# Layer 0's transposed features made in the last step of the first pipeline stage, in two buffers, instead of in the first step of the second stage

## The chip, the cores and the metric

The kernel runs on one core of a Trainium2 chip. The metric is the device time in microseconds (us), the median of several executions. The core has a matrix engine (PE), a vector engine (DVE), a scalar engine that evaluates functions from tables (ACT), GpSimd (POOL, used here only at the start), and queues that issue DMA transfers (SP's queue, in this kernel). Each engine works through its own list of instructions in the order in which the built program has them, and waits on semaphores where it needs another engine's result.

## The reference

Sixty-four graphs of 256 nodes with 128 features (`x`: 64 x 256 x 128) and dense 0/1 adjacency matrices (`adj`: 64 x 256 x 256) go through four message-passing layers, each followed by a residual and a layer norm:

```python
x = _layernorm(x + _L0_gnn_ref(x, adj, W, b))
x = _layernorm(x + _L1_gnn_ref(x, adj, ...))
x = _layernorm(x + _L2_gnn_ref(x, adj, ...))
x = _layernorm(x + _L3_gnn_ref(x, adj, ...))
```

Layer 0, the one the change is in, computes for each node the maximum over its neighbours of a pair term, with the weight matrix cut in two halves of 128 rows:

```python
W1, W2 = (W[:d], W[d:])
p = jnp.einsum('bnd,do->bno', x, W1 - W2)
q = jnp.einsum('bnd,do->bno', x, W2)
pre = p[:, :, None, :] + q[:, None, :, :] + b
h = jax.nn.relu(pre) * adj[..., None]
return jnp.max(h, axis=2)
```

Layer 1 has three projections with ELU (which needs Exp), two aggregations over the adjacency matrix and a Tanh. Layer 2 is a two-step graph convolution with ELU. Layer 3 forms a message for each pair of neighbours, with a layer norm (a square root) and a Gelu, and sums them. So four functions that ACT takes from tables occur: Exp, Tanh, Sqrt and Gelu.

## The kernel before, in words

The kernel does not visit all 256 x 256 pairs. It sorts each graph's neighbour lists into 40 "slots" of falling width, 4800 columns in all (`WIDTH`), and gathers a neighbour's vector by a matmul with a one-hot matrix `hot` (128 x 4800, for each of the two halves `h` of the nodes). Layer 0 takes the maximum over slots, layer 3 the sum. Because `hot` is a matrix of zeros and ones, the fp32 vectors are cut into three bf16 parts (`split3`, giving `q3` in layer 0 and `c3` in layer 3) that are multiplied one after the other into the same PSUM tile `bigp`. A second, general path stands behind a branch that these inputs do not take.

The work on one graph is cut into four stages, each a Python generator:

- `first`: loads `x0` and the adjacency `an`, sorts, makes `perm`, `permT`, `rank`, `lack` and, last, the one-hot matrix `hot`;
- `second`: layer 0 (`layer_0`), then layer 1 (`Shared.layer_1`);
- `third`: layer 2, then the first part of layer 3 (`c3`, `dT`, and the first four pieces by `sums_of`);
- `last`: the rest of layer 3 by pieces of 1024 columns (the fifth piece of each half has 704), the Gelu, the sums over slots, the final update and the store.

Four graphs are in flight at a time: while graph u is in `last`, u+1 is in `third`, u+2 in `second` and u+3 in `first`. The helper `together` interleaves the steps of the four generators (a step ends at each `yield`) in proportion to the numbers in `STAGES`. The Tile framework then schedules the recorded instructions onto the engines: it decides the order of each engine's list itself, within the data dependencies and the buffers that are free, so a moved step can shift every engine's order. All 64 graphs are unrolled; the order repeats from graph to graph in one "round" per graph. Function tables of ACT are loaded (`ACT_TABLE_LOAD`) wherever two functions of different tables follow each other in ACT's final order; the profile puts each load on the line of the function that needs it.

Names and lines that matter (numbers of the profile):

- `to_features` (L205, L207): two transposes on PE into a PSUM tile, then a copy by ACT into a tile in SBUF. It makes `xT_0`, `xT_1`, `xT_2` (layers 0, 1, 2; the profile shows all three as `xT`) and `x3T`.
- `layer_0`: L650 multiplies the features by `w0qp` (both weight halves); L497 to L500 cut q in three; L668 and L684 gather into `bigp`; L686 and L492 take the maximum into `lanes`; L691 ends a half (`total_m`), L694 and L695 transpose it (`mk`, twice a graph); L702 to L712 finish the layer.
- `layer_1`: feature copy, L221 and L228 the projections, L192 the Exp of `io` (two projections) and of `nd` (the third), L236 and L238 the aggregations, L241 their copy `ag`, L247 the update, L252 the Tanh.
- Layer 3: L731 gathers into `bigp`, L735 adds `dT` and gives `pre`, L739 squares, L746 sums the squares on PE, L748 copies `row`; two pieces of `row` go to DRAM and back as `vr` (L753, L765), L72 and L73 take the inverse root, L774 and L835 spread it as `rs_s`. In `last`, L846 multiplies `pre` by `rs_s`, L848 applies the Gelu, L492 and L488 fold the slots into `sums`, L867 to L869 multiply by the update weights, L872 copies the result (`ak`, once for each half), L877 brings it back to node order.
- Layer norms: L169 to L178 on DVE with the Sqrt of `rs` at L72 on ACT.
- Prologue: weights are loaded by `load` (L77) and in `prep` (L126 to L152); `sparse` counts slots with chains of small DVE instructions (L414 to L424), in scratch memory that is given back before the graphs' buffers are set up there.

## Time and profile before

| | |
|---|---|
| median of 3 runs | 5589.18 us (5588.3 to 5589.55) |
| the profiled execution | 5585.87 us, of which the trace spans 5583.8 |
| TensorE clock granted, mean | 0.876 |
| rounds | L798, once a graph, from 44.0 to 5423.0 us |
| one round by its stations (start, us) | `mk` 2604.88; layer 1's feature copy 2621.17; Exp of `io` 2626.39; second `ak` 2629.35; Tanh 2638.18; layer 0's feature copy 2640.81; `q` 2645.70; `lanes` 2649.08; next `mk` 2686.68 |

The round in the table and the one before it, by window (us busy; the windows run from the second `mk` of a graph to the first `lanes` of the next, and from there to the next second `mk`):

| window | length | PE | DVE | ACT | granted clock |
|---|---|---|---|---|---|
| 2519.04 to 2566.44 | 47.40 | 38.56 | 38.82 | 38.95 | 0.83 |
| 2566.44 to 2604.88 | 38.44 | 31.43 | 35.81 | 26.93 | 0.94 |
| 2604.88 to 2649.08 | 44.20 | 35.42 | 38.54 | 38.86 | 0.94 |
| 2649.08 to 2686.68 | 37.60 | 30.59 | 35.80 | 26.91 | 0.94 |

In the profile's lines, a group gives the line, the engine, the operation, the tile written and the tiles read with their shapes, the count, then the busy time in us, the mean of one in ns, and the idle time of the engine just before. A wait is given as the waiting engine, tile and line, then what it waited for, then the total in us, the count and the longest. A timeline row gives the start in us, the duration, the engine and line, and in brackets the idle time before it with what ended it. PEld is the load of a weight matrix into PE, which overlaps the matmuls. DVE is 92 to 95% busy between `lanes` and the next `mk`, and 82 to 87% busy between `mk` and `lanes`.

### The profile page before, as it was taken

The page shows a single profiled execution, that of the slowest core. Times are in us where ns is not written, and L with a number is a line of the kernel's source. Part 1 is how long each engine was busy: PE and PEld are TensorE (multiplying, and loading weights), DVE is VectorE, ACT ScalarE, POOL GpSimd, SP SyncE. Part 2 cuts the span into 40 slices and gives each one's busy share as a digit, 9 for nine tenths or more (in the row PEclk, how much of TensorE's full clock was granted, in tenths as well). Part 3 has the DMA queues.
Part 4 walks back from the last instruction along what each step waited for, and adds up shares of the span by engine and source line. Part 5 has one row for each costly group of instructions (what it writes and reads, how often), then busy time and mean ns, then how long its engine had stood idle before and what let it go on. Part 6 is the DMA issues. An engine that isn't in the chain of part 4 may idle for free.

```text
span 5583.8 us, 83622 instructions
## 1 busy us (share of the span) xinstructions
PE 4511.0 (81%) x27408; PEld 2487.9 (45%) x27408; DVE 4805.5 (86%) x14654; ACT 4218.5 (76%) x6465; POOL 2.0 (0%) x10
## 2 busy tenths in 40 slices
PE   5888888888788888887887888888888878888884
PEld 3444444444444444444444444444444444444442
DVE  7788888898888888888988888889888888888886
ACT  2777777777777777777777777777777777777776
POOL 0000000000000000000000000000000000000000
PEclk8888888888888888888888888888888888888886
DMA  0212222222222122222222222221222222212212
GB/s 24 65 59 72 67 63 66 72 65 66 66 65 70 60 72 67 63 66 74 63 66 67 70 66 61 69 67 63 71 70 63 66 67 70 66 59 71 64 59 76
DMA packets 292814, 365.17 MB, mean 65 GB/s; under 512 B 151952, under 2 KB 210448, under 8 KB 292368
## 3 DMA queue, kind: packets, MB, share of 16 engines
q1 hardware_dynamic: 292368, 359.73, 20.8%
q8 instruction: 218, 3.57, 0.3%
q14 instruction: 228, 1.87, 0.1%
HBM read 345.07 MB, written 14.53 MB: 64 GB/s over the span
## 4 chain that ended last, share of the span: by engine, by line
PE 42%; DVE 34%; ACT 17%; issue 5%; DMA 3%; SPq 0%; DVEq 0%; POOL 0%; ACTq 0%; POOLq 0%
PE bigp L731 8%; PE bigp L668 8%; DVE lanes L492 8%; DVE pre L735 6%; ACT L72 6%; DVE hot L628 5%; DVE sums L492 5%; PE mm L867 4%; DVE pre L846 3%; PE mm L746 3%; PE mm L877 2%; PE mm L817 2%; PE mm L294 2%; DMA rs_s<-scale_line 2%; ACT sums L848 2%
## 5 line engine op out<-in xcount | busy, mean ns | idle before, releaser
L668 PE MATMUL bigp<-hot,q 128*128 128x512 fp8e4 (+1 forms) x3840 | 1117.5, 391 | 206.2 <-DVE lanes L492 179.7
L731 PE MATMUL bigp<-hot,c 128*128 128x512 fp8e4 (+1 forms) x3840 | 1010.6, 395 | 136.0 <-DVE pre L735 77.1
L735 DVE TENSOR_TENSOR pre<-bigp,dT 128x512 f32<-128x512 f32 (+6 forms) x1664 | 841.4, 534 | 252.2 <-PE bigp L731 245.9
L739 ACT ACTIVATE sq<-pre 128x1024 f32<-128x1024 f32 (+1 forms) x640 | 636.6, 995 | 273.2 <-DVE rs L73 196.9
L492 DVE TENSOR_TENSOR lanes<-bigp,lanes 128x512 f32<-128x512 f32 (+6 forms) x1536 | 769.3, 501 | 12.2 <-ACT vr L72 2.9
L846 DVE TENSOR_TENSOR pre<-pre,rs_s 128x1024 f32<-128x1024 f32 (+1 forms) x640 | 734.4, 1148 | 35.6 <-DMA rs_s<-scale_line 34.5
L492 DVE TENSOR_TENSOR sums<-pre,sums 128x1024 f32<-128x1024 f32 (+6 forms) x1024 | 628.3, 614 | 11.6 <-ACT pre L848 11.2
L848 ACT ACTIVATE pre<-pre,be,g 128x1024 f32<-128x1024 f32 (+1 forms) x512 | 600.0, 1172 | 11.0 <-DVE pre L846 6.9
L731 PEld LDWEIGHTS <-c 128*128 128x128 bf16 x3840 | 346.2, 102 | 544.5 <-issue 268.1
L848 ACT ACT_TABLE_LOAD x447 | 573.5, 1283 | 7.9
L72 ACT ACT_TABLE_LOAD x447 | 573.5, 1283 | 7.9
L748 ACT ACTIVATE row<-mm,eps_t 128x256 f32<-128x256 f32 (+1 forms) x640 | 293.5, 459 | 361.9 <-PE mm L746 351.0
L668 PEld LDWEIGHTS <-q 128*128 128x128 bf16 x3840 | 309.6, 100 | 514.9 <-DVE lanes L492 186.5
L746 PE MATMUL mm<-sq,ones 128*32 128x256 f32 (+1 forms) x5120 | 436.5, 418 | 113.7 <-ACT sq L739 110.7
L628 DVE TENSOR_SCALAR hot<-rank 128x512 fp8e4<-128x512 bf16 (+5 forms) x1536 | 485.4, 345 | 0.0
L684 PEld LDWEIGHTS <-pick 42*128 42x128 bf16 x2944 | 154.5, 95 | 449.6 <-issue 435.2
L650 PE MATMUL mm<-w0qp,xT 128*128 128x256 f32 x256 | 130.0, 662 | 266.3 <-ACT xT L207 266.3
L867 PE MATMUL mm<-w3u,sums 128*128 128x128 f32 x2048 | 293.8, 287 | 44.9 <-DVE sums L492 44.9
L867 PEld LDWEIGHTS mm<-w3u,sums 128*128 128x128 f32 x2048 | 258.7, 195 | 75.9 <-PE bigp L731 39.6
L684 PE MATMUL bigp<-lack,pick 42*128 42x36 bf16 (+16 forms) x2944 | 275.8, 187 | 0.0
L746 PEld LDWEIGHTS mm<-sq,ones 128*32 128x32 f32 x5120 | 107.2, 115 | 352.5 <-ACT sq L739 162.0
L73 DVE RECIPROCAL vr<-vr 128x16 f32<-128x16 f32 (+1 forms) x320 | 79.5, 249 | 161.7 <-ACT vr L72 161.6
(227 smaller groups left out, 7319.0 us busy)
## 6 DMA issues: line engine op xcount, KB each, us to landing
rs_s<-scale_line SPq DMA_DIRECT2D x512, 512.0 KB
rs_s<-scale_line SPq DMA_DIRECT2D x128, 352.0 KB
an<-in_adj SPq DMA_DIRECT2D x64, 256.0 KB
x<-in_x SPq DMA_DIRECT2D x64, 128.0 KB
line<-row SPq DMA_DIRECT2D x512, 4.0 KB
out<-o SPq DMA_DIRECT2D x64, 128.0 KB
fu<-fulls SPq DMA_DIRECT2D x192, 4.0 KB
vr<-line SPq DMA_DIRECT2D x192, 8.0 KB
```

Of the source, the lines that this page charges most:

```text
L72: nc.scalar.activation(t, t, AF.Sqrt)
L492: nc.vector.tensor_tensor(lanes[:, :k, :w], src[:, i:i + k], lanes[:, :k, :w], op)
L628: nc.vector.tensor_scalar(hot[:, :, at:at + w], rank[:, :, :w], s0 + i + 1.0 - FAR, None, ALU.is_equal, saturate=False)
L668: nc.tensor.matmul(pt[:, :tl], q3[:, i, h], hot[:, h, t0:t0 + tl], start=i == 0, stop=False)
L684: nc.tensor.matmul(o_, l_, r_, start=False, stop=i == len(todo) - 1)
L731: nc.tensor.matmul(pt[:, :bl], c3[:, k, h], hot[:, h, t0 + b:t0 + b + bl], start=k == 0, stop=k == 2)
L735: nc.vector.tensor_add(block(pre[:, b:], n, w, at), block(pt, n, w, at), widen(dT[:, h, :w], n))
L739: nc.scalar.activation(sq[:, :tl], pre[:, :tl], AF.Square)
L746: nc.tensor.matmul(pr[q * Q:(q + 1) * Q, :tl // 4], ones[:, :Q], v4[:, :, q], start=True, stop=True)
L846: nc.vector.tensor_mul(pre[:, :tl], pre[:, :tl], rs[:, :tl])
L848: nc.scalar.activation(msg[:, :tl], pre[:, :tl], AF.Gelu, bias=be3, scale=g3)
L867: nc.tensor.matmul(pt[:, cols], lanes[:, k, cols], w3u[:, 1], start=k == 0, stop=False)
```

## The change

The call of `to_features` for layer 0 moves from the first step of `layer_0` to the end of `first`, after the last instructions that make `hot`. The `yield` that followed it goes away, so `second` has one step fewer, while the weights in `STAGES` stay. The tile `xT_0` gets the two buffers of its pool instead of one. To make room for the second buffer, the raw weights `w0` move from the pool of constants into `prep`, which is given back after the prologue; their load and the two DVE instructions that read them move with them, behind the loads and transposes of layer 1's weights.

```diff
-    w0 = load(l0_w.rearrange("(c p) o -> p c o", p=P), [P, 2, P], "w0")
     w0qp = consts.tile([P, 2, P], F32, name="w0qp")
-    nc.vector.tensor_copy(w0qp[:, 0], w0[:, 1])
-    nc.vector.tensor_sub(w0qp[:, 1], w0[:, 0], w0[:, 1])
...
             lambda t: [(w1_updT[:, c], t[:, c]) for c in range(3)],
         )
+        w0 = prep.tile([P, 2, P], F32, name="w0")
+        nc.sync.dma_start(w0, l0_w.rearrange("(c p) o -> p c o", p=P))
+        nc.vector.tensor_copy(w0qp[:, 0], w0[:, 1])
+        nc.vector.tensor_sub(w0qp[:, 1], w0[:, 0], w0[:, 1])
         w3 = prep.tile([P, 2, P], F32, name="w3")
...
             s["hot"] = hot
+            s["xT"] = sh.to_features(xn, "xT_0")
 
         def layer_0(s):
 
-            xn, hot, lack, lack_t, permT = (s[n] for n in ("xn", "hot", "lack", "lack_t", "permT"))
-            xT = sh.to_features(xn, "xT_0", 1)
-            yield
+            xn, xT, hot, lack, lack_t, permT = (s[n] for n in ("xn", "xT", "hot", "lack", "lack_t", "permT"))
             pq = psum()
```

## The prediction

> **What bounds the kernel now.** I read the page's parts on busy time, then the table-load groups of ACT (the groups by form: busy us, mean ns, idle before), then the waits, then a timeline of ACT at the place the change touches.

> ```profile
> PE 4511.0 (81%) x27408; PEld 2487.9 (45%) x27408; DVE 4805.5 (86%) x14654; ACT 4218.5 (76%) x6465; POOL 2.0 (0%) x10
> ...
> PE 42%; DVE 34%; ACT 17%; issue 5%; DMA 3%; SPq 0%; DVEq 0%; POOL 0%; ACTq 0%; POOLq 0%
> ```

> No engine is full; the chain that ended last hops between PE, DVE and ACT. So the time is set by waits between in-order queues, and an order of instructions matters as much as their number.

> ```profile
> L72 ACT ACT_TABLE_LOAD x447 | 573.5, 1283 | 7.9
> L848 ACT ACT_TABLE_LOAD x447 | 573.5, 1283 | 7.9
> ...
> L192 ACT ACT_TABLE_LOAD x133 | 170.6, 1283 | 2.4
> ...
> L252 ACT ACT_TABLE_LOAD x63 | 80.8, 1283 | 1.1
> L196 ACT ACT_TABLE_LOAD x61 | 78.3, 1283 | 1.1
> ```

> ACT changes its function table 1152 times (these five and one at L426), 1478 us in all, a third of its busy time: Sqrt (L72), Gelu (L848), Exp (L192, L196) and Tanh (L252) alternate.

> ```profile
> PEld mm L650 <- ACT xT L207: 277.5, 64, 4.8
> PE mm L650 <- ACT xT L207: 266.3, 64, 4.5
> DVE pre L735 <- PE bigp L731: 245.9, 308, 2.4
> ACT sq L739 <- DVE rs L73: 196.9, 62, 3.5
> ```

> The second line is what the change aims at: once for each of 64 graphs, layer 0's first matmul (L650) waits 266.3 / 64 = 4.2 us for the copy of its transposed features. The timeline shows why:

> ```profile
> 2636.39 0.47 ACT L748 ACTIVATE row<-mm,eps_t 128x256 f32<-128x256 f32 x1 [0.77 <-PE mm L746]
> 2636.88 1.28 ACT L252 ACT_TABLE_LOAD   x1
> 2638.18 0.42 ACT L252 ACTIVATE y<-y 128x256 f32<-128x256 f32 x1
> 2638.61 1.28 ACT L72 ACT_TABLE_LOAD   x1
> 2639.90 0.33 ACT L72 ACTIVATE rs<-rs 128x2 f32<-128x2 f32 x2
> 2640.14 0.77 ACT L739 ACTIVATE sq<-pre 128x704 f32<-128x704 f32 x1
> 2640.81 0.35 ACT L207 COPY xT<-mm 128x256 f32<-128x256 f32 x1
> ```

> PE finished the transposes at 2636.69 (timeline of PE), but the copy stands behind a Tanh, two table loads, two Sqrts and a Square.

> [...] L748 ends at 2636.86, the load starts at 2636.88, ends at 2638.16, and the Tanh starts at 2638.18. I go by the trace: 1.32 us a switch, plus about 0.1 us because neighbours without a load overlap by that much (the copy at 2640.81 starts 0.10 before the Square ends). [...]

> **The change, part by part.** No arithmetic is added: the built programs have the same number of PE, DVE, POOL and SP instructions. What changes is the order, since layer 0 has one step fewer and the first stage a longer last one, and the scheduler lays all engines out anew. (Line numbers here are those of before.) From the third or fourth graph on, both built orders repeat exactly. A round has 18 table loads before and 22 after; in the branch that runs, 1152 loads become 1383 (the other 134 belong to the branch not taken). 231 x 1.28 = 296 us of ACT work, about 330 with gaps. The rest of ACT's work is unchanged.

> *The aimed-at wait.* In the new order the transposes still stand directly ahead of L650 on PE, after all of the previous round, so they are not made early. On ACT their copy comes straight after the Tanh, ahead of the Sqrt load, the two Sqrts and the Square: 2640.81 would become about 2638.5, 2.3 of the 4.2 us. Also the first cut of q (L497) now stands ahead of the next Gelu. That is the gain, if everything before it came at its old time: 63 x 2.3 = 145 us.

> *Where the four loads lie.* Two lie in layer 2's end (Gelu of the 704 piece between the Sqrt of `vr` and that of `rs`). There ACT idles now (1.72 and 3.20 us around 2597 to 2601, in the timeline), and DVE takes up `rs` only after a dozen other instructions: I cost them at nothing; if that cover is gone, 2 x 1.4 = 2.8 us a round. The other two lie in layer 1. Before: Gelu load, Gelu 1024, feature copy, Gelu 704, then Exp load, Exp of `io`, Exp of `nd`. After: feature copy, Square, `ak`, Gelu load, Gelu 1024, Exp load, Exp `io`, Gelu load, Gelu 704, Square, Exp load, Exp `nd`. Queued behind are the second `ak` copy (L872), `ag` (L241), Tanh, and then the copy of the features itself.

> *The round laid out by hand*, with the durations of the round that begins with the second `mk` copy (L695, 2604.88, called 0). Each instruction of the new order starts when its queue and its inputs allow. Stations, us, before (trace) and after (worked out): layer 1's feature copy 16.3, 15.3; Exp of `io` 21.5, 21.7; end of the Gelu of the 704 piece 17.5, 25.0 (it waits for Exp of `io`, then a load of 1.28 and 0.97 of its own). Its sums on DVE need 3.0 more, with the `pre` additions that stand between (28.0); the sixteen passes of L867 on PE 2.3 (30.3); so the second `ak` is at 30.4 instead of 24.5. PE now does L236 and L238 first (2.3), then L323 and L877 (2.9, to 35.5); L746 0.6, ACT's `row` and Square, L247, L746, `row` (38.8), Tanh load: Tanh 40.1 instead of 33.3. Feature copy 40.5 instead of 35.9: later, although it has less ahead of it. L650 takes 2.1; q 43.0 instead of 40.8. Then come Sqrt load, `rs`, `aT`, `row`, Gelu load, Gelu, Sqrt load, `vr`, and only then `lanes`: 50.0 instead of 44.2. The first fold of `lanes` on DVE is at 51.3 instead of 45.2. DVE has by then done one L846 more (1.2) and `vr` (0.2), so 4.7 us of the 6.1 remain for the round.

> From `lanes` to the next `mk` the old round takes 37.6 us, DVE busy 35.8 of them (busy time by window). The new order leaves DVE 1.4 less there and ACT about 33 instead of 26.9: DVE still limits, so nothing is won back or lost.

> *From one round to all.* That round is a quick one (81.8). The copies L798 run from 44.0 to 5423.0 us, 63 intervals of 85.4; usual rounds lose most of the rest between `mk` and `lanes`, where the granted clock is 0.83 instead of 0.94 and PE is busy 38.6 instead of 35.4 us (windows of the round before). If ACT's longer queue hides all of that, the new round is 81.8 + 4.7 = 86.5, or 1.1 more; if none, 4.7 more. I take 3.0 as the middle: 63 x 3.0 = 189 us.

> *The prologue.* `w0` is now loaded 22 issues later on the SP queue (0.45 us each), after layer 1's weights, and its two DVE instructions (0.5 us) stand behind layer 1's transposed copies. Before, DVE filled the wait for these weights with the first chain of slot counts (L417: 0.31 + 1.07 + 5.73 + 3.28 = 10.4 us, from 1.5 to 12.3, while the first weights came at 15.0). In the new order that chain stands after the copies, ahead of the first graph's loads, which wait for this scratch memory to be freed (the issue at 31.95 waits for DVE, L440): 10.4 us once, nothing covers it. The later `w0` costs nothing by itself, as L650 needs it at 47.8.

> *Other edits.* Two buffers instead of one for the features, and the scratch place of `w0`, run no instruction: nothing.

> Sum: the profiled execution took 5585.9 us (span 5583.8 and 2.1 around it). 5585.9 + 189 + 10 = 5785; the median of the three runs is 3.3 higher, so 5788, which I round to 5790. Ends: 63 x 1.1 + 10 = 79, or 5668; 63 x 4.7 + 10 = 306, or 5895.

> **Rivals.** *Faster.* The wait goes and the loads hide: ACT idles 85.4 - 64.3 = 21 us a round (64.3 is its mean busy time over three rounds, by window), and a wait that ends last is shortened by 2.3; the chain passes at `q` L497 into L668. 5589 - 145 + 10 = 5454. Against: the two loads in layer 1 stand ahead of the very copy that should come sooner. 11 in 100.
> *A wash.* My reading of layer 1 is too strict, and what q gains is given back on DVE, where its second and third cuts now stand behind L846, which waits for the fetched scales: 5589 + 10 = 5599, give or take 40. 11 in 100.
> *All on the path.* ACT ends last everywhere: 4 x 1.4 = 5.6 us a round, 353 + 10: 5952. For: 33 busy us of 37.6 after `lanes` leave little slack. Against: the slack seen in layer 2. 10 in 100.
> *That the change doesn't do what it says* is in the forecast: the transposes still come last before L650.

> **Numbers.** Forecast 68 in 100 at 5790, by itself 5668 to 5895. The range reaches down over most of the wash and up into the last rival: 5590 to 5930; below lie 11 + 4, above 5. A measurement of this kernel can tell about 0.2% (11 us). Faster by more: 11 + 2 = 0.13; within: 0.05, from the wash; slower: 0.82.

> **What would show it.** About 1383 table loads in ACT, still of 1283 ns; the wait of L650 for the features cut to half or less; L798 at 87 to 90 us intervals; the second `ak` later against `mk` by some 6 us; the first `an` load some 10 us later. It is wrong if rounds are 85 or shorter though the loads are there: then the loads lay in slack.

## The result, and the profile after

The changed kernel takes 5624.19 us (median of 6 runs, 5616.19 to 5658.51); the kernel before, on the same chip, 5589.29. The ratio is 1.0072, 95% interval [1.0059, 1.0085]: slower by 0.7%, or 35 us, where 5790 was forecast. The profiled execution is the longest of the six (5658.51 us, span 5656.6), 72.6 us above the profiled one before. The ratios here and below use the runs within 1.5% of the fastest run of the same kernel; this leaves out only ten of the twenty runs of warm_after12.

Up to L640 the lines of the changed kernel are one higher than before (the feature copy L207 is L208, the Exp L192 is L193); from layer 0's first matmul on (L650) they are the same. From the page, busy time of each engine and the chain of work that ended last, by engine:

```profile
PE 4529.3 (80%) x27408; PEld 2565.6 (45%) x27408; DVE 4833.6 (85%) x14654; ACT 4536.5 (80%) x6696; POOL 1.8 (0%) x10
...
PE 43%; DVE 31%; ACT 18%; issue 6%; DMA 2%; SPq 0%; DVEq 0%; ACTq 0%
```

ACT is busy for 318 us more, the other two for 18 and 28. Where ACT's time went, from the groups by line (busy us, mean ns, idle before):

```profile
L848 ACT ACT_TABLE_LOAD x563 | 722.3, 1283 | 10.1
L72 ACT ACT_TABLE_LOAD x502 | 644.1, 1283 | 9.9 <-DMA vr<-line 0.9
L193 ACT ACT_TABLE_LOAD x253 | 324.6, 1283 | 4.6
L253 ACT ACT_TABLE_LOAD x62 | 79.5, 1283 | 1.1
```

With L197 (2) and L427 (1) these are the 1383 loads that the prediction counted. The waits (us in total, times, longest):

```profile
PE mm L694 <- DVE total_m L691: 353.4, 64, 5.6
DVE aT L276 <- PE mm L237: 219.9, 111, 4.5
...
PE mm L746 <- ACT sq L739: 186.8, 69, 6.7
...
PE mm L650 <- ACT xT L208: 139.3, 64, 3.0
...
DVE pre L735 <- PE bigp L731: 66.7, 134, 1.9
```

The wait that the change aims at fell from 4.2 to 2.2 us a round, and DVE's wait for L731 from 245.9 to 66.7 us. In their place L694 stands for 5.5 us a round (before: 1.7), L746 for 2.9 (1.7), and DVE has a new wait at L276.

The 72.6 us divide so. The copy L798 of the first graph starts at 54.86 us instead of 43.95: 10.9 us in the prologue. The 63 intervals of L798 average 86.32 us instead of 85.38: 63 x 0.98 = 62. The median run has 35 - 11 = 24 us for the rounds, 0.4 us each.

**What the average hides.** Before, nearly every round is 85.1 to 85.6 us long. After, rounds of 86.9 and 87.2 alternate (L798 intervals), with rounds of 81.8 and 84.7 between. Most are close to multiples of one time: 85.3 / 25 = 3.41; 81.8 / 24 = 3.41; (86.9 + 87.2) / 51 = 3.41. It is the step of TensorE's clock, as the traces show below. Here is a usual round of before and a round of after, each cut in four from the second `mk` copy (0 to 13 us, 13 to 36, 36 to 52, rest). Columns: window, its length, busy time of PE, weight load, DVE, ACT and POOL, then PEclk, the clock granted to PE, as a share of full speed.

```profile
2348.40:2361.40 13.00, 11.96 (x67) 8.97 (x66) 12.24 (x36) 12.70 (x18) 0.00 (x0) 0.90 0.29 80
2361.40:2384.40 23.00, 18.20 (x121) 11.56 (x119) 19.63 (x69) 16.40 (x24) 0.00 (x0) 0.93 0.14 34
2384.40:2400.40 16.00, 13.74 (x66) 5.69 (x67) 10.76 (x30) 13.60 (x26) 0.00 (x0) 0.68 0.37 113
2400.40:2433.70 33.30, 26.29 (x180) 12.44 (x179) 31.88 (x96) 23.19 (x36) 0.00 (x0) 0.94 0.22 62
```

```profile
2802.20:2815.20 13.00, 9.99 (x52) 6.65 (x50) 13.00 (x40) 12.07 (x17) 0.00 (x0) 0.88 0.13 32
2815.20:2838.20 23.00, 20.18 (x112) 14.31 (x111) 15.37 (x42) 15.90 (x21) 0.00 (x0) 0.78 0.13 39
2838.20:2854.20 16.00, 12.99 (x96) 6.55 (x95) 13.92 (x51) 14.09 (x25) 0.00 (x0) 1.00 0.28 79
2854.20:2888.20 34.00, 26.64 (x183) 12.19 (x175) 32.38 (x97) 29.21 (x44) 0.00 (x0) 0.94 0.31 91
```

Before, the clock is low in the third piece (0.68), right behind the wait of L650. After, that piece has the full clock, and the second has 0.78. In windows of 1 us the clock is 1.00 or 0.50 with at most one mixed window between, so 0.68 of 16 us means 10.2 us at half clock. Over 57 rounds of each profiled run (the sixth to the last but one), us at half clock in a round, by piece:

| kernel | mean round | 0 to 13 | 13 to 36 | 36 to 52 | after 52 |
|---|---|---|---|---|---|
| before | 85.3 | 2.6 | 3.4 | 10.1 | 4.2 |
| after, all | 86.6 | 5.6 | 7.5 | 2.0 | 4.1 |
| after, rounds of 86 (26) | 86 | 3.2 | 9.8 | 0.1 | 4.6 |
| after, rounds of 88 (23) | 88 | 9.1 | 6.4 | 3.9 | 3.7 |
| after, rounds of 82 (2) | 82 | 2.4 | 0 | 0 | 4.3 |
| before, round of 82 (1) | 82 | 2.1 | 0 | 3.4 | 4.6 |

(These rounds run from `mk` to `mk`; one of 86 and one of 88 make two L798 intervals of 87. Six more rounds of after are of 85 or 87.) In the middle pieces the stretches of a single round come as 0, 3.4, 6.8 or 10.2. Before, the usual round has 10.1 us more of them than the quick one and is 3.5 us longer (85.3 against 81.8). The change removed 8.1 us of half clock behind L650 and brought 4.1 behind another gap and 3.0 at the start of the round, where PE comes out of its wait at L694. The total fell, from 20.3 to 19.2 us, and yet the round grew by 1.3: what counts is how far each order is from its own quick round. Before is 10.2 us of half clock and 3.5 us of time above it, after 12.5 and 4.8, so a microsecond at half clock goes with 0.34 and 0.39 us of the round. With the half clock at its least, both orders take 81.8.

The other gap, with its cause, in the timelines of ACT and of PE for the same round (start, duration, engine, line, instruction; in brackets the idle time before and who ended it):

```profile
2818.28 1.28 ACT L848 ACT_TABLE_LOAD   x1
2819.58 1.24 ACT L848 ACTIVATE pre<-pre,be,g 128x1024 f32<-128x1024 f32 x1
2820.84 1.28 ACT L193 ACT_TABLE_LOAD   x1
2822.14 0.63 ACT L193 ACTIVATE elu_e<-io 128x512 f32<-128x512 f32 x1
2822.67 0.46 ACT L748 ACTIVATE row<-mm,eps_t 128x256 f32<-128x256 f32 x1
2823.15 1.28 ACT L848 ACT_TABLE_LOAD   x1
2824.44 0.98 ACT L848 ACTIVATE pre<-pre,be,g 128x704 f32<-128x704 f32 x1
2825.32 1.04 ACT L739 ACTIVATE sq<-pre 128x1024 f32<-128x1024 f32 x1
```

```profile
2826.42 1.08 PE L746 MATMUL mm<-sq,ones 128*32 128x256 f32 x8 [2.82 <-ACT sq L739]
...
2912.55 0.64 PE L746 MATMUL mm<-sq,ones 128*32 128x256 f32 x8 [2.82 <-ACT sq L739]
```

Two of the new loads are among the three that stand ahead of the Square, and PE waits 2.82 us for it. The second PE line is the same place one round on, a round of 81.8 us: the wait is the same 2.82, but the matmuls behind it take 0.64 us and not 1.08. With the same wait that round is no longer than before's quick one; what differs is whether the half clock follows.

**Which gaps slow the clock.** In the traces of before and after the granted clock changes only on a grid with a step of 3.41 us: of the 392 and 362 stretches of one clock, all but the last of each are a whole number of steps long. (The expectations call a step a window.) These are the two PE gaps of 2.82 us cut on that grid, in the columns of above: the one that ends at 2826.42, then the one that ends at 2912.55.

```profile
2822.42:2825.84 3.42, 1.18 (x8) 0.48 (x6) 3.35 (x9) 3.39 (x5) 0.00 (x0) 1.00 0.00 1
2825.84:2829.25 3.41, 2.83 (x16) 1.98 (x16) 3.39 (x16) 3.38 (x5) 0.00 (x0) 0.50 0.00 0
2829.25:2832.66 3.41, 3.41 (x15) 2.53 (x14) 0.34 (x2) 0.61 (x3) 0.00 (x0) 0.50 0.03 4
```

```profile
2907.76:2911.17 3.41, 1.97 (x11) 0.87 (x9) 3.41 (x8) 3.37 (x5) 0.00 (x0) 1.00 0.00 1
2911.17:2914.58 3.41, 1.98 (x19) 1.27 (x19) 3.34 (x14) 3.38 (x6) 0.00 (x0) 1.00 0.02 5
2914.58:2918.00 3.42, 3.42 (x22) 2.99 (x22) 1.83 (x9) 2.94 (x6) 0.00 (x0) 1.00 0.03 4
```

The first gap leaves PE busy for 1.18 of the 3.42 us of a step, and the next steps have half clock, three in all. The second is split by the grid: PE is busy for 1.97 and 1.98 us of the two steps, over half of each, and the clock stays. Nearly all steps of the 57 rounds at full clock agree. In before, PE is less than half busy in 170 of them, and half clock follows all 170; it follows none of the other 915. In after it follows 154 of 161, and 5 of the other 965. At this wait alone, after has 53 gaps of 2.7 to 2.9 us: 48 leave a step with PE at most 0.39 busy, and half clock follows every one; 5 are split with at least 0.54 in both steps, and it follows none. The gap of 4.3 us at L650 before is longer than a step: in each of the 57 rounds it leaves a step with PE at most 0.23 busy, and half clock follows every one. But a gap need not be as long as a step: 2.82 us was enough in those 48 cases of 53, and 2.2 us, what is left of the wait of L650 in after, in 26 of 56. For how long the clock then stays low (mostly 3.4 to 10.2 us) I have no such rule.

### The profile page after: what moved, and what is told of

Same layout as the page of the kernel before. It is cut to its first block, busy times and chain, and to the rows that moved or that the text cites. A ratio compares the mean times of both kernels' runs of the same rounds, so it can differ in the third digit from the quotient of the medians.

```text
span 5656.6 us, 83740 instructions
## 1 busy us (share of the span) xinstructions
PE 4529.3 (80%) x27408; PEld 2565.6 (45%) x27408; DVE 4833.6 (85%) x14654; ACT 4536.5 (80%) x6696; POOL 1.8 (0%) x10
## 4 chain that ended last, share of the span: by engine, by line
PE 43%; DVE 31%; ACT 18%; issue 6%; DMA 2%; SPq 0%; DVEq 0%; ACTq 0%
PE bigp L668 8%; PE mm L867 6%; DVE lanes L493 5%; PE mm L746 5%; DVE hot L629 5%; DVE pre L735 4%; PE bigp L731 4%; DVE sums L493 4%; ACT L848 3%; DVE pre L846 3%; ACT L193 3%; ACT sq L739 2%; PE mm L237 2%; PE mm L702 2%; PE mm L877 2%
## 5 line engine op out<-in xcount | busy, mean ns | idle before, releaser
L668 PE MATMUL bigp<-hot,q 128*128 128x512 fp8e4 (+1 forms) x3840 | 1084.5, 374 | 137.4 <-DVE lanes L493 80.9
L731 PE MATMUL bigp<-hot,c 128*128 128x512 fp8e4 (+1 forms) x3840 | 917.6, 375 | 13.4 <-DVE pre L735 12.8
L735 DVE TENSOR_TENSOR pre<-bigp,dT 128x512 f32<-128x512 f32 (+6 forms) x1664 | 843.0, 536 | 71.8 <-PE bigp L731 66.7
L739 ACT ACTIVATE sq<-pre 128x1024 f32<-128x1024 f32 (+1 forms) x640 | 640.9, 1001 | 226.3 <-DVE rs L73 137.3
L846 DVE TENSOR_TENSOR pre<-pre,rs_s 128x1024 f32<-128x1024 f32 (+1 forms) x640 | 731.5, 1152 | 24.5 <-DMA rs_s<-scale_line 23.5
L848 ACT ACT_TABLE_LOAD x563 | 722.3, 1283 | 10.1
L72 ACT ACT_TABLE_LOAD x502 | 644.1, 1283 | 9.9 <-DMA vr<-line 0.9
L746 PE MATMUL mm<-sq,ones 128*32 128x256 f32 (+1 forms) x5120 | 475.7, 420 | 187.2 <-ACT sq L739 186.8
L848 ACT ACTIVATE pre<-pre,be,g 128x1024 f32<-128x1024 f32 (+1 forms) x512 | 602.5, 1177 | 15.5 <-DVE pre L846 9.0
L731 PEld LDWEIGHTS <-c 128*128 128x128 bf16 x3840 | 344.0, 100 | 413.3 <-issue 91.0
L668 PEld LDWEIGHTS <-q 128*128 128x128 bf16 x3840 | 297.5, 98 | 475.0 <-issue 164.2
L748 ACT ACTIVATE row<-mm,eps_t 128x256 f32<-128x256 f32 (+1 forms) x640 | 290.8, 454 | 217.0 <-PE mm L746 216.7
L867 PE MATMUL mm<-w3u,sums 128*128 128x128 f32 x2048 | 395.8, 349 | 18.3 <-DVE sums L493 17.9
L867 PEld LDWEIGHTS mm<-w3u,sums 128*128 128x128 f32 x2048 | 342.2, 249 | 83.7 <-DVE sums L493 46.3
L694 PE MATMUL mm<-ident,total_m 128*128 128x128 f32 x256 | 68.4, 360 | 353.4 <-DVE total_m L691 353.4
L193 ACT ACT_TABLE_LOAD x253 | 324.6, 1283 | 4.6
L746 PEld LDWEIGHTS mm<-sq,ones 128*32 128x32 f32 x5120 | 114.8, 114 | 372.1 <-ACT sq L739 219.9
```

The lines of the kernel that those rows point to most:

```text
L72: nc.scalar.activation(t, t, AF.Sqrt)
L193: nc.scalar.activation(e, t, AF.Exp)
L668: nc.tensor.matmul(pt[:, :tl], q3[:, i, h], hot[:, h, t0:t0 + tl], start=i == 0, stop=False)
L731: nc.tensor.matmul(pt[:, :bl], c3[:, k, h], hot[:, h, t0 + b:t0 + b + bl], start=k == 0, stop=k == 2)
L735: nc.vector.tensor_add(block(pre[:, b:], n, w, at), block(pt, n, w, at), widen(dT[:, h, :w], n))
L739: nc.scalar.activation(sq[:, :tl], pre[:, :tl], AF.Square)
```

## The experiments

Theories. *Clock*: the old order loses time to the half clock behind L650; the change takes that away and pays by opening other gaps. *Loads*: the change pays with 231 more table loads on the path. *Prologue*: the place of `w0` carries the cost.

| run | median us | ratio to before, 95% |
|---|---|---|
| w0_late | 5599.87 | 1.0020 [1.0013, 1.0027] |
| move_only | 5610.01 | 1.0045 [1.0028, 1.0062] |
| after_keep_step | 5623.29 | 1.0069 [1.0052, 1.0086] |
| before_one_table | 5363.35 | 0.9599 [0.9583, 0.9615] |
| after_one_table | 5394.34 | 0.9651 [0.9634, 0.9667] |
| warm_before12 | 5527.93 | 0.9897 [0.9880, 0.9913] |
| warm_before20 | 5506.08 | 0.9850 [0.9834, 0.9867] |
| warm_after12 | 5572.39 | 0.9908 [0.9883, 0.9932] |
| after_add_pool | 5683.00 | 1.0172 [1.0155, 1.0189] |
| warm_before20_8 | 5725.33 | 1.0251 [1.0234, 1.0269] |
| warm_after_sums | 5734.82 | 1.0236 [1.0185, 1.0286] |

**The change in two halves.** w0_late is before with only the move of `w0`; its instruction order within the rounds is that of before.

```diff
-    w0 = load(l0_w.rearrange("(c p) o -> p c o", p=P), [P, 2, P], "w0")
...
+        w0 = prep.tile([P, 2, P], F32, name="w0")
+        nc.sync.dma_start(w0, l0_w.rearrange("(c p) o -> p c o", p=P))
```

> The kernel before with one part of the change alone: the load of layer 0's weight and its two conversions stand in the preparation behind layer 1's weights, the features stay where they were. If the shifted instruction order makes the rounds longer and w0's place only delays the first stage (10.9 us in the trace of after), the median is 5589 + 11 = 5600 us and the rounds stay at 85.3 us. If the later w0 costs nothing because later work takes up the slack, 5589.

Measured +12.0 us, rounds 85.4. move_only is the other half: `w0` stays, the features move, with one buffer. Its order within the rounds is that of after.

```diff
             s["hot"] = hot
+            s["xT"] = sh.to_features(xn, "xT_0", 1)
...
-            xT = sh.to_features(xn, "xT_0", 1)
-            yield
```

> The other part alone: the features are made at the end of the first stage and the step is dropped, with one buffer, and w0 stays where it was. Theory that the two costs simply add: the median excess of 34.9 us less the prologue's 10.9, so 5613 us, with single runs anywhere from 5605 to 5650 and rounds of 85.5 to 86.5 us. Rival: the place of w0 carried nearly all of it, and the move itself is neutral: 5589 +- 5. Second rival: one buffer instead of two holds the copy back in the first stage and brings a wait there: above 5630.

Measured +22.2 us. The halves add to 34.2 of 34.9, so the second buffer is worth nothing that these runs can tell (the interval of move_only is 10 us to either side), and the rounds carry about 22 us, 0.35 each.

**Are the loads the price?** after_keep_step is after with the dropped `yield` put back at the head of layer 0.

```diff
             xn, xT, hot, lack, lack_t, permT = (s[n] for n in ("xn", "xT", "hot", "lack", "lack_t", "permT"))
+            yield
             pq = psum()
```

> The change, but with the step (the yield) at the head of layer 0 kept, so that layer 0 advances as it did before while the features are made a stage earlier. This order has 1288 activation-table loads in the program instead of 1517, so the two extra loads in layer 1 and the two in layer 2's end are gone. If the extra loads (4 x 1.28 us a round) are what the change pays with, this is faster than the kernel before: the rounds are 85.3 us or less, 5480 to 5600 us. If the length of a round is set by TensorE's half-clock stretches, the loads matter only where they open a gap on TensorE, and the rounds lie near 81.9 (5385 us) or 85.3 (5600 us), whichever number of 3.41-us windows fits, with little in between.

The trace has 1154 loads (1288 less the 134 of the branch not taken) in place of 1383, yet the time is that of the change. So the extra loads come with the dropped step, but they are no needed part of the cost. This run has a third order, though, with little half clock in the middle (1.0 and 3.8 us) and rounds of 85.6 on average, so it has slower spots of its own. Its rounds are of 84, 85 and 87 us, not of the two lengths that were expected: not every order keeps to whole steps of the clock. The cleaner test keeps each kernel's order: after it is laid out, the four functions are replaced by Identity, so the results are no longer those of the network. The replaced instructions take about as long as before (L848: 1172 ns on average in before, 1176 in before_one_table; ACT's busy time falls by 1496 us, of which the 1151 loads that went make 1477).

```diff
+            if type(i).__name__ == "InstActivation" and i.func in (AF.Gelu, AF.Exp, AF.Tanh, AF.Sqrt):
...
+                todo[k] = mybir.InstActivation(func=AF.Identity, **kw)
```

> The kernel before in its own instruction order, with Gelu, Exp, Tanh and Sqrt computed as Identity (this changes the values of the whole network, nothing else), so that 1154 table loads of 1.283 us go and one stays. It is the base for the run of the change done the same way. By itself: ScalarE gets 18 x 1.283 = 23 us of a round back; if the waits for ScalarE set the round, 3 to 8 us a round go, 5100 to 5400 us; if DVE and TensorE's clock set it, it stays within a window of 3.41 us: 5375 to 5589.

> The changed kernel in its own order, with the same four functions as Identity: its 1383 loads become one. The theory that the change pays with its 229 extra loads: this run stands above the same edit of the kernel before by the prologue alone, 11 to 12 us. The theory that the new order itself (what is queued ahead of what, and which gaps open on TensorE) costs what the shorter wait for the feature copy earns: it stays 20 us or more above, or falls to a different side altogether, since the gaps move; a difference under 11 us would mean that order without loads is a gain.

Without loads both are faster by 225 and 230 us, and the change is still 31.0 us above. Its first L798 is 11.2 us later there (53.65 against 42.46), so 20 us remain in the rounds, as with the loads. So the difference does not need the loads: taken out of both kernels, they leave it where it was. (That the loads do nothing in the full kernels isn't shown; two of them stand ahead of the gap at L746.) The gap only changes its owner. In after_one_table PE no longer waits much for the Square at L746 but for DVE's sums beside it:

```profile
PE mm L694 <- DVE total_m L691: 353.2, 64, 5.6
PE mm L867 <- DVE sums L493: 189.7, 63, 14.5
```

and the half clock in 13 to 36 is still 4.3 us, where before_one_table has 1.3 there and 8.9 behind L650. The rounds of before_one_table keep to 81.9, 24 times 3.41.

**The half clock behind L650 by itself.** 12 or 20 dummy matmuls keep PE busy while it waits for the copy (twelve of them took 2.75 us in warm_before20; 216 ns is the median from one start to the next of the 512-column matmuls of L668 and L731 in before). They write layer 0's own PSUM tile, which the real matmul then overwrites; after the first 260 us, DVE's and ACT's order is that of before.

```diff
             pq = psum()
+            for _ in range(12):
+                nc.tensor.matmul(pq, ones_b, hot[:, 0, :512], start=True, stop=True)
```

> The kernel before with 12 dummy bf16 matmuls of 512 columns written into layer 0's PSUM tile ahead of its real matmul (which overwrites them), so that TensorE is busy for about 2.6 us of the some 4 us in which it waits for the feature copy; nothing else moves. Theory of the clock: the wait itself costs little, the 10 us at half clock that follow it cost 3.4 us a round; with the dummies they go and a round is 81.9 us, 24 windows of 3.41 us in place of 25: 5589 - 63 x 3.4 = 5375 us. Rival, that only the wait for the copy counts and the slow clock is covered by other engines: no gain, 5589, up to 5589 + 63 x 2.6 = 5750 if the dummies run late and hold back the real matmul.

> The kernel before with 20 dummy matmuls ahead of layer 0's first real one in place of 12 (about 4.3 us of work for a wait of about 4.2 us); the rest of the order is that of before. If what counts is that no gap on TensorE long enough to lower its clock is left there, this is as fast as with 12 or a little faster, 5490 to 5530 us. If the dummies' own time begins to count, it is slower than with 12 by up to 8 x 0.216 x 63 = 109 us.

Both are faster, by 60 and 82 us, though not by the 215 that a whole step of 3.41 us in each round would give. A round of 81.8 us of warm_before20, in the same four pieces:

```profile
2394.00:2407.00 13.00, 11.72 (x66) 8.73 (x65) 12.24 (x36) 12.72 (x18) 0.00 (x0) 0.92 0.24 81
2407.00:2430.00 23.00, 20.48 (x140) 12.72 (x139) 20.89 (x75) 18.17 (x28) 0.00 (x0) 1.00 0.18 56
2430.00:2446.00 16.00, 13.79 (x86) 5.89 (x84) 12.74 (x32) 15.33 (x28) 0.00 (x0) 1.00 0.24 82
2446.00:2475.80 29.80, 22.77 (x161) 11.16 (x161) 28.39 (x89) 19.76 (x31) 0.00 (x0) 0.92 0.25 69
```

The third piece now has the full clock. Over 57 rounds it has 2.4 us at half clock where before had 10.1; the rounds average 84.2 (L798), and not 81.8, because in 27 of the 57 a stretch of 3.4 us stays in each of the two middle pieces. So the slow clock behind this wait cost at least 1.2 us a round; the real matmuls tell it directly, in before and then in warm_before20 (where L652 is before's L650):

```profile
2386.39 2.08 PE L650 MATMUL mm<-w0qp,xT 128*128 128x256 f32 x4 [4.30 <-ACT xT L207]
```

```profile
2430.37 1.12 PE L652 MATMUL mm<-w0qp,xT 128*128 128x256 f32 x4
```

warm_before20 beats both kernels, by 1.5% against before. The same dummies in the changed kernel:

> The changed kernel with the same 12 dummies at the same place, where the wait is only some 2 us; this shifts the order a little (1455 table loads in the program where the change has 1517). If the half-clock stretch after this wait has already gone by the change itself, the dummies gain little or nothing: 5610 to 5640 us. If the clock after this wait still matters as in the kernel before, 60 us are gained: 5565.

The median is 52 us under the change, near the second number, but it stands for runs from 5494 to 5642 (its ratio to the median of before is 0.997), and the order had shifted too, so this run does not tell the two theories apart. Its profiled run shows why it scatters: 22 of 57 rounds are 82, with no half clock in 13 to 36; 29 are 86 or 88, with 10.2 or 6.8 us of it. PE's wait for the Square is there as before (187.4 us in total). The rounds stay in one pattern or the other for several at a time.

**Is DVE's new wait the price?** The addition L276 writes the tile that layer 1's matmul L237 reads, and it stands early in DVE's queue. Put on GpSimd, it leaves ACT's, PE's and the rest of DVE's order as it was.

```diff
                 blk = aT[:, h, h * P:(h + 1) * P]
-                nc.vector.tensor_add(blk, blk, ident)
+                nc.gpsimd.tensor_add(blk, blk, ident)
```

> The changed kernel with layer 2's in-place addition of the identity to the transposed adjacency (two small operations a round) on GpSimd in place of DVE; the order on TensorE and ScalarE and the rest of DVE's is that of the change. In the trace of the change DVE stands 3.4 us a round before this addition, since layer 1's matmul still reads the same tile, and everything behind it on DVE stands too. If this wait sets the round, it goes: 1 to 3.4 us a round, 5410 to 5560 us. If TensorE, slowed after its own gap, ends later anyway (the next operation of the path on DVE waits for the matmul at the end of the layer above), the wait only moves there: 5624 +- 15 us.

The wait moved, as the rival said, to another entry of DVE's queue, where after waits 9.4 us in total; but the time, 5683, is neither of the two expected (waits of after_add_pool):

```profile
DVE dinv L73 <- ACT dinv L72: 260.9, 62, 4.5
```

None of the 60 longest waits is for the additions on GpSimd. The medians differ by 59 us; the profiled runs differ by 28, and 24 of these lie in the rounds: 53 of 57 are 86 or 88 (after: 49), and hardly a quicker one is left. Where the rest comes from isn't shown.

**Filling other gaps.** warm_before20_8 adds 8 dummies ahead of the transposes L694; warm_after_sums puts 14 ahead of L867 for the second half in the changed kernel.

```diff
                 pt = psum()
+                for _ in range(8):
+                    nc.tensor.matmul(pt, ones_b, hot[:, 0, :512], start=True, stop=True)
                 for hk in range(H):
                     nc.tensor.transpose(pt[:, hk * P:(hk + 1) * P], mx[:, hk * P:(hk + 1) * P], ident)
```

> The kernel before with the 20 dummies ahead of layer 0's matmul and 8 more ahead of each pair of transposes of the folded maxima, where TensorE waits 1.7 us at the end of the round and runs at half clock for 6 to 8 us across it. If that stretch is worth as much as the first one, 63 x 1 to 3.4 us more: 5290 to 5440 us. If DVE's folds end the round and TensorE only follows, nothing: 5506 +- 15 us, or slower by up to 2 x 8 x 0.216 x 63 = 218 us where the dummies hold back the transposes.

> The changed kernel with 14 dummies ahead of the matmuls that take the second half's folded sums: there TensorE idles 2.8 us in the rounds of 87 us (ScalarE is late with a square, or DVE with the sums) and runs at half clock for up to 10 us behind it, and not in the rounds of 81.8 us. The order shifts somewhat with it (1460 table loads in the program for 1517). If this gap is what the change pays with, more rounds come near 81.8: 5430 to 5570 us. If the gap is harmless, 5624 +- 20 us, or up to 14 x 0.216 x 63 = 190 us slower.

Both lost. The first has 16 dummies more a round; PE's busy time grew by 233 us over warm_before20, 3.6 us a round, and the round by 3.4 (87.6 against 84.2): there PE was not waiting long enough to hide them. (DVE's order had shifted a little too.) The second missed its gap: the wait for the Square (L746, 187.4 us in total) stands ahead of the dummies and remained, and the matmuls behind them only came later. So it says nothing on the gap of 2.8 us; whether filling that gap would turn the change into a gain stays open.

## Why the prediction was wrong

- *The prologue* was right: 10.4 us forecast, 10.9 in the trace, 12.0 as the median of w0_late.
- *The loads* were counted right (1383, 1283 ns each). But the cost does not need them: taken out of both kernels, they leave the difference of the rounds as it was. So the direction came out right, but not for the reason given.
- *The wait of L650* fell to 2.2 us, about the 1.9 forecast.
- *The round laid out by hand* matches a round of after that carries half clock: in the one that begins at 2714.2 the Exp of `io` is at 21.7 and `lanes` at 49.8, as forecast (21.7, 50.0). That is partly luck: this round has a clock of 0.64 in its first 13 us, where the one it was laid out on has 0.92, and it ends at 87.9, not 86.5. The layout's 4.7 us were laid against before's quick round, and there they fail. In after's quick round (2888.3) the stations are, with the forecast in brackets: layer 1's feature copy 13.5 (15.3), `io` 20.0 (21.7), second `ak` 27.6 (30.4), Tanh 36.4 (40.1), q 38.3 (43.0), `lanes` 45.1 (50.0). So 1.8 of the 4.9 us are missing at the first station already. L650, costed at 2.1 us, its duration at half clock, takes 1.1 at full. At `lanes` 0.9 us of the loss is left, and at the end of the round nothing: 81.8 both before and after.
- *From `lanes` to the next `mk`* the forecast held. It had this part end at 86.5 - 50.0 = 36.5 us, as DVE had done 1.4 us of its work by then; after's quick round took 36.7, and the average went from 38.5 to 37.4, with DVE busy for 35.3 us where it was 35.8. What went wrong lies ahead of `lanes`.
- **The step that failed** is the cost of the new order from `mk` to `lanes`, and with it *From one round to all*: "I take 3.0 as the middle." The hand layout had `lanes` at 50.0 us instead of 44.2, 4.7 us a round when all of it shows; in the quick rounds it was 45.1 and the round no longer at all. The average term of 3.0 measured 0.98 a round in the profiled run (62 us) and about 0.4 in the median one (24 us), instead of 189 us. I had seen the granted clock of 0.83 between `mk` and `lanes` in the usual rounds, and treated it as a loss that ACT's longer queue might or might not hide. It had a cause, the gap of 4.2 us at L650 (half clock follows it in 57 rounds of 57), which is the very thing that the change shortens: warm_before20 shows the loss and its cause with DVE's and ACT's order untouched. So that loss leaves with the wait. What the rounds of after lose against their own quick ones goes with the half clock behind the new order's gaps, not with the queue positions that I added up; no run that fills those gaps shows it by itself.
- The rival of a wash (5599, give or take 40) held the time, but that its reason holds isn't shown; that of all loads on the path (5952) fell with the time itself.

Which rounds of after are slow is told by where the gap of 2.82 us falls on the clock's grid (53 gaps of 53). What stays open is why the rounds come back to the bad places in most cases, and whether the changed kernel would be the faster one without this gap.

## What to carry to other kernels

Look at the granted clock stage by stage before costing a wait on TensorE: here gaps of 2.2 to 4.3 us were followed by half clock (26 times of 56 and 57 of 57), which slows what comes next too (L650 took 2.08 us, and 1.12 at full clock in warm_before20), and a change that shortens the gap can take that away as well. When moving work shortens one wait, ask where TensorE will next stand idle for that long, since the loss can simply move there. A few dummy matmuls in the waiting tile's own PSUM place are a cheap test, and here a gain of 1.5%; put where PE waits only 1.7 us, they cost nearly their full time (3.4 us a round for 3.6).
